# Softmax denominators of a two-layer graph attention kernel: summed over queries in the exp's accumulator instead of over keys by accumulating transfers

## The chip, the cores and the metric

One core of a Trainium2 chip runs the whole program. Times are microseconds of device time; the time of a kernel is the median of its runs. TensorE, VectorE, ScalarE, GpSimd and the sync engine each work through their own queue in order and wait for one another by semaphores.

## The reference

The input is x, 16 graphs of 1024 nodes with 256 features, and an integer adjacency of 1024 x 1024 for each graph, symmetric and with ones on the diagonal. Two layers follow, each added to its input. The first, cut to what matters here:

```python
normed = layer_norm(x, gamma1, beta1)                       # h = relu(layernorm(x)) comes in as x
qkv = normed.reshape(b_, n_, H, HD).transpose(0, 2, 1, 3)   # 8 heads of 32
scores = jnp.einsum('bhqd,bhkd->bhqk', qkv, qkv) * scale
masked = jnp.where(adj_matrix[:, None, :, :] > 0, scores, -jnp.inf)
attn = jax.nn.softmax(masked, axis=-1)
out = jnp.einsum('bhqk,bhkd->bhqd', attn, qkv)
x = x + out
return x + gelu(layer_norm(x, gamma2, beta2) @ W1 + b1) @ W2 + b2
```

Queries, keys and values are the same array, so the scores are symmetric, and with a symmetric adjacency the masked scores are too. The second layer is a graph attention with one head (leaky ReLU of bilinear logits, masked, softmax, weighing, two projections, ELU). Only the first layer's softmax is touched by the change.

## The kernel before, in words

All is float32 but the masks (fp8). There is a fast path, written out in `fast_path`, and a `general_path` that runs afterwards only if flags gathered on the chip (`seen`, `dens`, `not_bounded`) say that the fast path's assumptions did not hold. The fast path leaves out the maximum of the softmax.

*Attention of the first layer* (`attention`, L969). Each graph is a batch b of 32 blocks, in the order query half qh (2 of 512 queries), group g (2 of four heads), key tile kt (8 of 128 keys). `scores` (L974) puts keys on the partitions and queries on the free axis: for a block, sixteen small matmuls (L990) fill two PSUM tiles of 128 x 1024, one for two heads. VectorE adds the mask and moves each tile to SBUF (L1011), ScalarE takes the exp in place (L1014), one instruction of 1024 elements per tile. In batch 0 TensorE adds the mask of the first tile itself (matmuls with an identity, L571), and ScalarE reads that tile from PSUM. One block later `weigh` (L1022) multiplies by the values (L1027) into one PSUM tile `o` of 128 (four heads of 32 features) x 512 queries, gathered over the eight key tiles.

*Denominators.* The sum that is needed for a query runs over keys, that is, over partitions and key tiles. The e tiles of key tile 0 are kept as accumulators (`acc`), and for the others `add_up` (L1048) issues a transfer from GpSimd's queue that adds e to acc in SBUF (L1051). In batch 0 the odd key tiles are summed apart by VectorE (L1038). After the last key tile, `total` (L924) sums acc over the partitions with matmuls by ones (L929), ScalarE copies the sums out (L937), `invert` (L942) turns them by small matmuls (L947) so that queries lie on the partitions, and VectorE takes reciprocals (L951). `finish` (L954) then transposes the weighed values (L961), multiplies by the reciprocals (L963), and GpSimd adds the result to the residual h (L967). `go_on` (L1068) moves these steps on by one each block through the lists `weighed`, `summed` and `totalled`.

*The rest of a batch* (`rest`, L1114: the MLP with its Gelu, the second layer, the stores) is a chain of generators that run during the attention of the next batch, so that TensorE always alternates between attention blocks and pieces of the previous batch. Its 128-wide matmuls go through `matmul` (L566), which splits the stationary operand into four quarters of 32 columns.

*What sets the order.* The order of instructions on each engine is written out in Python. Streams (L1435 to L1492) each yield a place on a common axis, in batches (one block is 1/32), and the loop at L1494 always runs the stream with the smallest place. `clock` is a planned time in microseconds; `defer` (L758) puts an instruction behind others by a due time on that clock, and `turns` holds transposes that wait for a free PSUM tile (`make_turns`, L913). `stream_p` prepares the first statistics for the MLP (`prepare`, L1092), `stream_m` loads and transposes the masks of a query half before it begins (`turn_masks`, L890). At the end of `fast_path` each engine's instructions are tied to this order.

The line numbers are those of the kernel before. The functions that the diff touches:

Of the kernel before, what the change touches and what calls it, by code (L numbers as in the profile page):

```python
# [12 lines left out]
I32 = mybir.dt.int32  # L13
AF = mybir.ActivationFunctionType
# [480 lines left out]
def fast_path(  # L495
# [54 lines left out]
    ep = pool("ep", 5)  # L550
    accp = pool("accp", 2)
# [36 lines left out]
    def convert_mask(b, t, halves):  # L588

        m = mqp.tile([P, N], FP8, tag="mq", name=f"mq_{b}_{t}")  # L590
        for i, a in enumerate(halves):
            nc.vector.tensor_scalar(
                m[:, i * QW : (i + 1) * QW], a, 0.0, NEG8, op0=ALU.is_le, op1=ALU.mult, saturate=False
            )
        return m
# [4 lines left out]

    each_head = const.tile([P, GH], F32, name="each_head")
    nc.vector.tensor_copy(each_head, ident[:, ::HD])
# [57 lines left out]
    seen = const.tile([P, 4], F32, name="seen")  # L660
# [114 lines left out]
    def prologue(b, st):  # L775
# [61 lines left out]
        if b == 0:  # L837
# [3 lines left out]
            mqs = midp.tile([P, 2 * TPH, N], FP8, tag="mid", name="mq_0")  # L841
# [48 lines left out]
    def turn_masks(b, qh, st):  # L890
# [7 lines left out]
        mq = convert_mask(*raw)  # L898
        raw = fetch_mask(b, ts[1])
        for i in range(TPH):  # L900
            yield
            nc.sync.dma_start_transpose(pairs[:, :, i * P : (i + 1) * P], mq.bitcast(BF16))
            if i + 1 < TPH:
                mq = convert_mask(*raw)
            if i + 2 < TPH:
                raw = fetch_mask(b, ts[i + 2])


# [4 lines left out]
    def make_turns():  # L913
        room = 3 - open_sums[0] - bool(summed or totalled) if open_sums[0] else 100
# [7 lines left out]
    scored, weighed, summed, totalled = [], [], [], []  # L922

    def total(b, qh, g, os, accs):  # L924

        den = ps_tile([P, QW], f"den_{b}_{g}_{qh}")
        for j in range(GH):
            for acc in accs:
                nc.tensor.matmul(  # L929
                    den[j * HD : (j + 1) * HD, :],  # L930
                    ones,
                    acc[j // 2][:, j % 2, :],
                    start=acc is accs[0],
                    stop=acc is accs[-1],
                )
        ds = tmpp.tile([P, QW], F32, tag="w2", bufs=3, name=f"ds_{b}_{g}_{qh}")
        nc.scalar.copy(ds, den)  # L937
        totalled.append((b, qh, g, ds, os))

    finished = {}  # L940

    def invert(b, qh, g, ds, os):  # L942

        pt = ps_tile([P, TPH, GH], f"ptds_{b}_{g}_{qh}")
        for t in range(TPH):
            for c in range(0, P, HD):
                nc.tensor.matmul(  # L947
                    pt[c : c + HD, t, :], ds[:, t * P + c : t * P + c + HD], each_head, start=True, stop=True
                )
        rl = smallp.tile([P, TPH, GH], F32, tag="rl", name=f"rl_{b}_{g}_{qh}")  # L950
        ready = defer(1.0, lambda: nc.vector.reciprocal(rl, pt))  # L951
        turns.append((1, lambda: finish(b, qh, g, rl, ready, os)))

    def finish(b, qh, g, rl, ready, os):  # L954
# [7 lines left out]
        ot = tmpp.tile([P, TPH, GH, HD], F32, tag="w2", bufs=3, name=f"ot_{b}_{g}_{qh}")  # L962
# [6 lines left out]
    def attention(b, st):  # L969
        va, kT = st["va"], st["kT"]  # L970

        def scores(qh, g, kt):  # L974
# [24 lines left out]
            if b == 0 and kt % 2:  # L999

                odd = midp.tile([P, 2, 2, QW], F32, tag="mid", name=f"odd_{g}_{qh}_{kt}")
            for i in range(2):
                if b == 0 and kt % 2:
                    e = odd[:, i]
                elif kt == 0:
                    e = accp.tile([P, 2, QW], F32, tag=f"acc{i}", name=f"acc_{b}_{g}_{qh}_{i}")
                else:
                    e = ep.tile([P, 2, QW], F32, tag="e", name=f"e_{b}_{g}_{qh}_{kt}_{i}")
# [5 lines left out]
                weights = lambda e=e, masked=masked: nc.scalar.activation(e, masked, AF.Exp, scale=SCALE)  # L1014
# [4 lines left out]
        acc = {}  # L1019


        def weigh(qh, g, kt, es):  # L1022
# [11 lines left out]
            if b == 0 and kt % 2:  # L1034

                if kt > 1:
                    for n, (e, w) in enumerate(zip(es, odds[g, qh])):
                        defer(1.0 + 2.5 * n, lambda e=e, w=w: nc.vector.tensor_add(e, e, w))  # L1038
                odds[g, qh] = es
            if kt == NT - 1:  # L1040
                c = tmpp.tile([P, QW], F32, tag="w2", bufs=3, name=f"os_{b}_{g}_{qh}")
                nc.vector.tensor_copy(c, o)
                weighed.append((b, qh, g, c, [s[g, qh] for s in (sums, odds) if s]))

        sums, odds = {}, {}


        def add_up(qh, g, kt, e, i):  # L1048
            if b == 0 and kt % 2:
                return  # L1050
            nc.gpsimd.dma_start(sums[g, qh][i], e, accum_op=ALU.add)  # L1051

        units = [(qh, g, kt) for qh in range(NQH) for g in range(NG) for kt in range(NT)]
        for u in units:
# [3 lines left out]
            rest_of_weights()  # L1058
            qh, g, kt = u
            if kt == 0:  # L1060
                sums[g, qh] = es
            else:
                for i in range(2):
                    defer(2.0 + 1.5 * i, lambda u=u, e=es[i], i=i: add_up(*u, e, i))
            scored.append((weigh, (*u, es)))
            yield

    def go_on():  # L1068
        was_weighed, was_summed, was_totalled = weighed[:], summed[:], totalled[:]
        for l in (weighed, summed, totalled):  # L1070
            l.clear()
# [493 lines left out]
```

## Time and profile before

| | us |
|---|---|
| median of 3 runs | 3475.63 (3471.41 to 3486.16) |
| the profiled execution, own time | 3465.53 |
| its span, first to last instruction | 3463.8 |
| TensorE busy | 3421.5 |
| VectorE busy | 2751.4 |
| ScalarE busy | 1857.5 |
| GpSimd busy | 1416.9 |
| accumulating transfers L1051: 864, 453 MB | GpSimd 756.2 |
| exps L1014, 128 x 1024: 852 on e, the others on acc or in batch 0 | 1.057 each |
| scores L990 and weighing L1027 (8192 and 4096 matmuls) | 577.3 and about 550 |
| summing L929 and turning L947 of the denominators (544 and 2048 matmuls) | 76.0 and 29.8 |

The profile is of one execution. An engine's busy time is the union of its instructions' durations. TensorE's durations overlap and their ends are modelled, so its price for a piece of work is better read from start to start in the timeline, where each row has its start, its length, engine, line, output and inputs, shape and count, and in brackets the idle time before it with what ended it. PEld is TensorE's loading of weights, which runs beside its matmuls. The granted TensorE clock was 0.998 of full speed. Batch 0's attention lies between 22 and 146 us, and from batch 1 on a batch takes about 211 us.

### The profile page before, as it was taken

What the parts mean: (1) busy time and instruction counts of PE and PEld (TensorE: products, weight loads), DVE (VectorE), ACT (ScalarE), POOL (GpSimd) and SP (SyncE); (2) the same over time, 40 slices, a digit from 0 to 9 for tenths busy, and PEclk for the clock granted to TensorE, in tenths of its full rate; (3) what the DMA queues carried; (4) which work ended last, traced back from release to release, by engine and by line L of the source; (5) the groups of instructions that cost most, each with busy time, mean ns of one, the idle gap of its engine ahead of it and who ended that gap; (6) DMA issues with size and microseconds to landing.
All of it is one profiled execution on the core that took longest, in us unless ns stands there. A gap on an engine that the chain in (4) does not pass through costs nothing. (4 is left out here: it accounts for less than half of the span.)

```text
span 3463.8 us, 119015 instructions
## 1 busy us (share of the span) xinstructions
PE 3421.5 (99%) x52478; PEld 1644.7 (47%) x52478; DVE 2751.4 (79%) x5194; ACT 1857.5 (54%) x2184; POOL 1416.9 (41%) x1708
## 2 busy tenths in 40 slices
PE   7999999999999999999999999999999999999998
PEld 2344444444444444444444444444444444444477
DVE  6888788787878878888887887878878788887754
ACT  5555555555555555555555555555555555555522
POOL 4443443434444344443444434344343443433220
PEclk9999999999999999999999999999999999999999
DMA  8799989999899998999999899998999989899730
GB/s 195 154 183 181 185 164 194 177 193 185 164 185 176 185 187 169 184 171 191 189 177 186 166 189 179 188 187 168 186 178 193 186 163 184 170 193 180 153 64 14
DMA packets 281902, 598.56 MB, mean 173 GB/s; under 512 B 94880, under 2 KB 130080, under 8 KB 281376
## 3 DMA queue, kind: packets, MB, share of 16 engines
q0 software_dynamic: 124416, 453.04, 71.5%
q1 hardware_dynamic: 156672, 137.56, 15.9%
q8 instruction: 414, 6.78, 0.8%
q14 instruction: 112, 0.92, 0.1%
q10 hardware_dynamic: 288, 0.26, 0.0%
HBM read 104.21 MB, written 16.78 MB: 35 GB/s over the span
## 5 line engine op out<-in xcount | busy, mean ns | idle before, releaser
L1014 ACT ACTIVATE e<-e 128x1024 f32<-128x1024 f32 x852 | 895.9, 1057 | 947.6 <-DVE e L1011 715.3
L1051 POOL DMA_DIRECT2D acc<-e x864 | 756.2, 891 | 1447.4 <-DMA acc<-e 664.6
L1011 DVE TENSOR_TENSOR e<-s,mk 128x1024 f32<-128x1024 f32 x852 | 1004.0, 1218 | 180.1 <-PE s L990 148.4
L990 PE MATMUL s<-kT 32*64 32x512 f32 x8192 | 577.3, 615 | 2.9 <-DVE odd L1011 2.9
L1027 PE MATMUL o<-e,va 128*32 128x512 f32 x3456 | 462.9, 606 | 2.1 <-ACT e L1014 2.1
L571 PE MATMUL pa<-gw,e 128*32 128x258 f32 x7648 | 454.3, 380 | 0.6 <-issue 0.6
L571 PE MATMUL lg<-fT,uT 128*32 128x256 f32 x7680 | 448.5, 379 | 0.0
L571 PE MATMUL ph<-yT,w 128*32 128x256 f32 x7808 | 448.5, 379 | 0.0
L571 PE MATMUL po<-w,hid 128*32 128x256 f32 x7680 | 440.5, 379 | 0.0
L571 PEld LDWEIGHTS ph<-yT,w 128*32 128x32 f32 x7808 | 259.8, 110 | 197.7 <-issue 42.5
L571 PEld LDWEIGHTS po<-w,hid 128*32 128x32 f32 x7680 | 250.2, 110 | 209.1 <-issue 61.6
L571 PEld LDWEIGHTS lg<-fT,uT 128*32 128x32 f32 x7680 | 258.4, 110 | 190.1 <-issue 38.9
L571 PEld LDWEIGHTS pa<-gw,e 128*32 128x32 f32 x7648 | 249.9, 110 | 202.5 <-issue 49.9
L1287 ACT ACTIVATE e<-e,shift 128x512 f32<-128x512 f32 x256 | 183.0, 717 | 186.0 <-DVE e L1286 161.2
L1281 DVE SCALAR_TENSOR_TENSOR e<-lg,gw,mk 128x256 f32<-128x256 f32 x512 | 223.2, 478 | 71.6 <-PE lg L571 61.1
L1184 DVE TENSOR_TENSOR hid<-ph,b1c 128x512 f32<-128x512 f32 x256 | 175.6, 688 | 85.6 <-PE ph L571 74.2
L1027 PEld LDWEIGHTS o<-e,va 128*32 128x32 f32 x3456 | 68.8, 108 | 354.0 <-issue 219.9
L1286 DVE SCALAR_TENSOR_TENSOR e<-e 128x512 f32<-128x512 f32 x256 | 196.6, 768 | 8.8
L1014 ACT ACTIVATE acc<-acc 128x1024 f32<-128x1024 f32 x124 | 131.0, 1057 | 129.0 <-DVE acc L1011 124.6
L990 PEld LDWEIGHTS s<-kT 32*64 32x64 f32 x8192 | 120.6, 130 | 162.8 <-issue 105.0
L1011 DVE TENSOR_TENSOR acc<-s,mk 128x1024 f32<-128x1024 f32 x124 | 146.1, 1218 | 20.8 <-PE s L990 20.6
L815 POOL TENSOR_TENSOR nrm<-nrm,g 128x256 f32<-128x256 f32 x128 | 113.3, 885 | 60.9 <-DVE nrm L749 60.9
(146 smaller groups left out, 3817.9 us busy)
## 6 DMA issues: line engine op xcount, KB each, us to landing
acc<-e POOLq DMA_DIRECT2D x864, 512.0 KB, 6.2
adj<-in_adj_dram SPq DMA_DIRECT2D x248, 256.0 KB, 5.6
h<-in_x_dram SPq DMA_DIRECT2D x64, 256.0 KB, 6.3
xb<-in_x_dram SPq DMA_DIRECT2D x128, 128.0 KB, 4.2
out_dram<-z SPq DMA_DIRECT2D x128, 128.0 KB, 4.0
adj<-in_adj_dram SPq DMA_DIRECT2D x4, 512.0 KB, 7.1
mk<-mq SPq DMA_TRANSPOSE x128, 6.4
w<-in_L_gnn_W_dram SPq DMA_DIRECT2D x2, 1024.0 KB, 9.6
```

The lines of the kernel that those rows point to most:

```text
L571: nc.tensor.matmul(out[c : c + HD], lhsT[:, c : c + HD], rhs, start=start, stop=stop)
L815: nc.gpsimd.tensor_mul(nrm, nrm, g1)
L990: nc.tensor.matmul(sc[j // 2][c : c + P // 2, j % 2, :], kT[r, g, kt * P + c : kt * P + c + P // 2], kT[r, g, qs], start=j >= by_pe, stop= ...
L1011: nc.vector.tensor_tensor(e, masked, mb, op=ALU.add)
L1014: weights = lambda e=e, masked=masked: nc.scalar.activation(e, masked, AF.Exp, scale=SCALE)
L1027: nc.tensor.matmul(o[j * HD : (j + 1) * HD, :], va[:, kt, (g * GH + j) * HD : (g * GH + j + 1) * HD], es[j // 2][:, j % 2, :], start=(kt = ...
L1051: nc.gpsimd.dma_start(sums[g, qh][i], e, accum_op=ALU.add)
L1184: nc.vector.tensor_tensor(hid[:, f0 : f0 + 2, :], ph, b1c[:, f0 : f0 + 2].unsqueeze(2).to_broadcast([P, 2, CW]), op=ALU.add,)
L1281: nc.vector.scalar_tensor_tensor(e[:, j, :], lg[:, j, :], gw[:, kt, D : D + 1], st[c // 2][:, kt // 2, qs, kt % 2], op0=ALU.add, op1=ALU.add,)
L1286: nc.vector.scalar_tensor_tensor(e, e, ALPHA, e, op0=ALU.mult, op1=ALU.max)
L1287: ready = defer(2.5, lambda: nc.scalar.activation(e, e, AF.Exp, bias=shift))
```

## The change

*Sums over queries.* Because the masked scores are symmetric, the denominator of node n is also the sum over all queries of row n, with n as a key. A row is a partition of an e tile, and its sum over 512 queries is what ScalarE's accumulator can give with the exp. The exp of a tile (two heads) is therefore cut into two instructions of 512 elements, one for each head, with `accum_out` into a column of a new tile `den` (one per batch: query half, key tile, head). `total`, `add_up`, the acc tiles, the odd sums of batch 0 and the matmuls of `invert` are gone. The new `invert` adds the two query halves' columns on VectorE and takes reciprocals. As a node's sum needs both query halves, the finishes of the first query half now come in the second one: for each group, after its key tiles 3 and 7 of the second half, `invert` handles the nodes of query half 0 and 1, and `close` puts `finish` on the list of turns. The weighed values of the first half are kept until then (`w2`, 3 buffers to 5).

*Check of symmetry.* `turn_masks` keeps the fp8 masks with queries on the partitions (`mq`) beside the transposed ones (`mk`). `compare_masks` subtracts one from the other on GpSimd, for the pairs of tiles on and under the diagonal of query halves, 12 instructions of 128 x 512 per batch; VectorE ORs the bits of each result into `uneven` as int32 (128 x 256). At the end the maximum byte of `uneven` goes into the flags, and a difference leads to `general_path`. `stream_k` sets the compares' places: from 0.02 to 0.20 of a batch after each query half begins.

*Places and rooms.* `prepare` moves from 0.85 and 0.90 to 0.91 and 0.935, the start of `rest` from 0.94 to 0.96 and its run from 0.98 to 0.99; the last batch closes in two steps instead of four; e tiles get 6 buffers instead of 5 and the accumulators' four go.

```diff
-    ep = pool("ep", 5)
-    accp = pool("accp", 2)
+    ep = pool("ep", 6)
+    denp = pool("denp", 2)
...
+    seen = const.tile([P, 6], F32, name="seen")
+    nc.gpsimd.memset(seen[:, 5:6], 0.0)
+    uneven = const.tile([P, QW // 2], I32, name="uneven")
+    nc.gpsimd.memset(uneven, 0)
...
-        mq = convert_mask(*raw)
+        mq = st["mq", qh] = mqp.tile([P, TPH, N], FP8, tag="mq", name=f"mq_{b}_{qh}")
+        convert_mask(mq[:, 0], *raw)
...
+    def compare_masks(b, qh, st):
+        for half in range(qh + 1):
+            for i in range(TPH):
+                kt = qh * TPH + i
+                odd = smallp.tile([P, QW], BF16, tag="odd", bufs=2, name=f"odd_{b}_{qh}_{half}_{i}")
+                key = st[half][:, kt // 2, :, kt % 2]
+                query = st["mq", qh][:, i, half * QW : (half + 1) * QW]
+                nc.gpsimd.tensor_tensor(
+                    odd.rearrange("p (u v x) -> p u v x", u=2, v=2),
+                    key.rearrange("p (u v x) -> p u v x", u=2, v=2),
+                    query.rearrange("p (u x v) -> p u v x", u=2, v=2),
+                    op=ALU.subtract,
+                )
+                o = odd.bitcast(I32)
+                defer(3.0, lambda o=o: nc.vector.tensor_tensor(uneven, uneven, o, op=ALU.bitwise_or))
+                yield
...
-        room = 3 - open_sums[0] - bool(summed or totalled) if open_sums[0] else 100
+        room = 3 - open_sums[0] if open_sums[0] else 100
...
-    def total(b, qh, g, os, accs):
...
-                nc.tensor.matmul(
-                    den[j * HD : (j + 1) * HD, :],
-                    ones,
-                    acc[j // 2][:, j % 2, :],
...
-        nc.scalar.copy(ds, den)
...
-    def invert(b, qh, g, ds, os):
...
-                nc.tensor.matmul(
-                    pt[c : c + HD, t, :], ds[:, t * P + c : t * P + c + HD], each_head, start=True, stop=True
-                )
...
-                weights = lambda e=e, masked=masked: nc.scalar.activation(e, masked, AF.Exp, scale=SCALE)
+                def weights(e=e, masked=masked, i=i):
+                    for j in range(2):
+                        n = g * GH + 2 * i + j
+                        nc.scalar.activation(
+                            e[:, j], masked[:, j], AF.Exp, scale=SCALE, accum_out=den[:, qh, kt, n : n + 1]
+                        )
...
-                        defer(1.0 + 2.5 * n, lambda e=e, w=w: nc.vector.tensor_add(e, e, w))
...
-            nc.gpsimd.dma_start(sums[g, qh][i], e, accum_op=ALU.add)
+        def close(qh, g):
+            turns.append((1, lambda: finish(b, qh, g, *rl[g, qh], os[g, qh])))
+        def invert(qh, g):
+            r = smallp.tile([P, TPH, GH], F32, tag="rl", name=f"rl_{b}_{g}_{qh}")
+            ts, hs_ = slice(qh * TPH, (qh + 1) * TPH), slice(g * GH, (g + 1) * GH)
+            def f():
+                nc.vector.tensor_tensor(r, den[:, 0, ts, hs_], den[:, 1, ts, hs_], op=ALU.add)
+                nc.vector.reciprocal(r, r)
+            rl[g, qh] = r, defer(2.5, f)
...
+            if qh == NQH - 1 and kt % TPH == TPH - 1:
+                invert(kt // TPH, g)
+                if kt < NT - 1:
+                    close(kt // TPH, g)
...
-        for _ in range(4):
+        for _ in range(2):
...
-            place = b + 0.98
+            place = b + 0.99
...
-                yield b + 0.85 + 0.05 * c
+                yield b + 0.91 + 0.025 * c
...
-            yield b + 0.94
+            yield b + 0.96
...
+    def stream_k():
+        for b in range(B):
+            for qh in range(NQH):
+                yield from spread(
+                    compare_masks(b, qh, states[b]), TPH * (qh + 1), b + 0.5 * qh + 0.02, b + 0.5 * qh + 0.2
+                )
```

## The prediction, made before the changed kernel ran

> **What bounds the kernel now.** I read the page's shares first. TensorE is busy 99% of the span, and the slices show it so from the second one to the last but one.
>
> ```profile
> PE 3421.5 (99%) x52478; PEld 1644.7 (47%) x52478; DVE 2751.4 (79%) x5194; ACT 1857.5 (54%) x2184; POOL 1416.9 (41%) x1708
> PE   7999999999999999999999999999999999999998
> ```
>
> A busy TensorE could still be one that waits inside modelled durations, so I went to the timeline and measured from start to start. Over all runs of matmuls of one kind followed by the same next kind, smallest and median distance agree (scores L990 to the weighing L1027: 1.044 us in both, over 511 places). The excess over the median adds up to 21 us in the whole program, 16 of it before 165 us, that is in batch 0. From batch 1 on TensorE waits for nobody: what is taken off its queue shortens the program, and what is added elsewhere is free until it uses up a slack. These rows of the timeline in mid-program price the work that goes:
>
> ```profile
> 1686.60 1.06 PE L1027 MATMUL o<-e,va 128*32 128x512 f32 x8
> ...
> 1687.49 1.04 PE L929 MATMUL den<-acc,ones 128*32 128x512 f32 x8
> ...
> 1688.35 1.91 PE L571 MATMUL po<-w,hid 128*32 128x256 f32 x32
> ...
> 1694.68 1.07 PE L1027 MATMUL o<-e,va 128*32 128x512 f32 x8
> ...
> 1695.57 0.42 PE L947 MATMUL ptds<-each_head,ds 128*32 128x4 f32 x30
> ...
> 1695.86 3.64 PE L571 MATMUL ph<-yT,w 128*32 128x256 f32 x62
> ```
>
> The denominators' sum (L929) holds the queue from 1687.49 to 1688.35, 0.86 us; turning them (L947) from 1695.57 to 1695.86, 0.29 us. In both cases the weighing before keeps its own 0.88 us.
>
> The slack that the change spends is that between the last exp of a block (one query half, one group of four heads, one key tile) and its weighing. The tightest place repeats in every batch; here it is once, in block 28 of 32 of a batch:
>
> ```profile
> 1810.24 2.35 DVE L1011 TENSOR_TENSOR e<-s,mk 128x1024 f32<-128x1024 f32 x2
> ...
> 1811.54 2.19 ACT L1014 ACTIVATE e<-e 128x1024 f32<-128x1024 f32 x2 [3.31 <-DVE e L1011]
> ...
> 1814.11 0.16 PEld L1027 LDWEIGHTS o<-e,va 128*32 128x32 f32 x8 [0.81 <-ACT e L1014]
> ```
>
> The exps end at 1813.73, the weighing starts 0.4 us later. I took this distance for all 480 blocks of batches 1 to 15: median 2.3 us, a tenth under 0.45 us (blocks 28 and 29 about 0.4, block 21 0.65, block 6, behind a Gelu and its table load, 0.8). The scores' own slack (VectorE's mask add, L1011, frees their PSUM tile) has a median of 2.6 us.
>
> **What the Trainium skill says.** ScalarE: Activation LUTs, section What ACT_TABLE_LOAD costs, gives an activation with immediate scale and bias as 186 ns + 0.833 ns per element, and back-to-back ones as overlapping by about 93 ns. The trace agrees: 1057 ns for 1024 elements (1039 by the page), and neighbours overlap by about 100 ns. The same page, What it computes, names an accumulator output, but no price. GPSIMD Engine Reference, section 3.1, has a two-input elementwise operation at about 2.6 cycles per element at 1.2 GHz; for 512 elements that is an estimate of 1.1 us and a start. L967, 128x512, takes 1.45 us on average here, 1.29 in the median. SBUF — State Buffer, section Who interferes with whom, says that a VectorE instruction with two SBUF inputs and a GpSimd instruction that reads SBUF hold one another up for the whole instruction. L1286, of that kind, shows it: shortest 691 ns, mean 768.
>
> **The change part by part.**
> *TensorE.* L929 has 512 + 32 matmuls, 68 groups of eight: 68 x 0.86 = 58.5 us. L947 happens 64 times: 64 x 0.285 = 18.2 us. Together 77 us, all on the path. I don't use the page's busy sums (70.6 + 5.4 + 29.8 = 106), because they count overlapping ends twice. Everything else on TensorE stays.
> *ScalarE.* 1024 exps over 1024 elements become 2048 over 512, each with an accumulator output, and 64 copies L937 (36 us) go. A half costs 1057 - 512 x 0.833 = 630 ns, or 0.53 from start to start. Reading the accumulator has no row: from below nothing, from above one smallest instruction, the 128x1 copies of L693 at 159 ns, without any overlap and with a little for the write, 0.2 us. I take 0.06 per half (159 less the overlap of 100), and the full 0.16 after the last. A block's four halves then end 0.63 + 3 x 0.59 + 0.16 = 2.56 us after the first begins, against 2.0 to 2.19 now: about 0.5 us later. Against the slack of the 480 blocks, 0.5 us makes 7 us of waits, mostly in blocks 28 and 29; blocks that lose L929 become shorter, for which I add 3: +10 us. ScalarE's busy time rises by some 1024 x (4 x 0.59 / 2 - 1.0) less 36, to about 2.0 ms of 3.4, so it isn't the bound.
> *GpSimd and the DMA queues.* The 864 accumulating transfers (L1051, 0.88 us each on GpSimd's queue, 453 MB, 71.5% of the DMA engines) go: worth nothing directly, since TensorE waited for them for 1.4 us in all. What they hid or crowded only gets earlier. In come 192 compares, 128x512 with fp8 inputs and four-dimensional patterns. No such row is there; I take L967's 1.3 to 1.5 us and keep 0.7 (the 128x256 rows) and 5 us as ends. GpSimd falls from 1417 us to 1417 - 757 + 192 x 1.45 = 940.
> *VectorE.* In: 192 ORs of 128x256, L1333's 496 ns, 95 us; 64 adds of 128x16 beside the 64 reciprocals that stay, at L951's 248 ns, 16 us. Out: 24 adds L1038, 30 us. Net +81, to 2832 us of about 3400 (83%). The OR is a new wait: behind it stand the mask adds, and behind these the exps and TensorE. It is put 3 us of planned time after its compare, and in most places several VectorE instructions lie between. The ORs fall into blocks 1 to 7 and 17 to 23, of which 3, 6 and 21 have under 1.1 us of slack: I put 0.4 us for each of 15 batches, +6 us; bounds 0 and 95 (every OR on the path).
> *Moved.* The first query half's finishes (four transposes, 0.59 us of TensorE; L963, 0.68 of VectorE; L967, 1.45 of GpSimd) go to blocks 20 and 28, the second's to 25 and to block 1 of the next batch, now without the steps of summing and turning in between. The first MLP statistics go from 0.85 and 0.90 of a batch to 0.91 and 0.935; the next stage's two x loads on the sync queue go with it from 0.94 to 0.96. A finish at block 28 leaves one block (about 6 us) for 0.66 + 0.68 + 1.45 = 2.8 us, and statistics and normalizing have two more before their transposes: nothing; if that cover were gone, at most the 2.8 us once per batch. The new add of the two halves' sums waits on VectorE for the block's last exp; 2.5 to 3.3 us of other VectorE work stand between mask add and this add: nothing.
> *Batch 0.* Here exps read PSUM directly, and TensorE's next block waits for them: half exps cost up to 0.4 x 32 = 13 us. Against that, 30 us of VectorE adds and the transfers disappear, and 16 us of present waits with them at best. I set it to nothing, bounds -16 to +13.
> Sum: -77 + 10 + 6 + 0 = -61 us. The profiled execution took 3465.5 us (span 3463.8), so 3404.5; the runs shown have a median of 3475.6, 0.29% above it, which gives 3414 us.
>
> **Rivals.**
> 1. *ScalarE's accumulator is dear.* At 0.83 us per half (0.63 + 0.2, no overlap) the block's exps end 1.1 us later, and the same slacks give 39 us of waits; with batch 0 at its worse end: -77 + 39 + 6 + 13 = -19, 3457 us on the runs' scale. For it: no row prices that read. Against: the 128x1 row is only 159 ns.
> 2. *Slower: VectorE waits for GpSimd's compares.* Place: the second half of each batch's attention, where eight compares are spread over some six blocks. In seven blocks there (46 us in the trace) GpSimd has 16 us of work besides the transfers, which leaves 30 us, 3.7 per compare. Beyond that each OR stops VectorE, with all mask adds behind it. At 5 us per compare: 8 x 1.3 = 10.4 us a batch, less 2.3 of slack, x 15 = +120, so -77 + 10 + 120 + 6 = +59, 3535 us. It decides from about 4.5 us per compare. For: unpriced types and patterns. Against: L967's 1.29 us for as many elements.
> 3. *All of it and more.* Nothing of ScalarE shows, and batch 0's waits vanish: -77 - 16 = -93, 3382 us.
> 4. *The compare doesn't recognise the symmetry*, and the general path runs as well: thousands of us. The two patterns name the same pairs when I work them out, so 1%.
>
> **How the numbers follow.** Chances: forecast 0.60, dear accumulator 0.18, slower by the compares 0.11, more than the sum 0.10, general path 0.01. A measurement of this kernel tells about 0.5% from no change, 17 us. Faster: 0.60 + 0.10 and the better half of rival 1, 0.80; same: the rest of rival 1, 0.08; slower 0.12. The range runs from near rival 3 to just past rival 1: 3386 to 3462.
>
> **What would show it.** No L929 or L947, weighing followed after 0.88 us by the next kind everywhere. Half exps of 0.6 to 0.65 us with a small row between; if their distance from start to start exceeds 0.75 us, rival 1 gains, and waits of the weighing on ScalarE appear in blocks 28, 29 and 21. Compares over 3.7 us, or VectorE idle before the OR for GpSimd, would mean rival 2. It is wrong at the root if TensorE, with these 77 us gone, shows new gaps in every block.

## The result, and the profile after

The changed kernel takes 3421.8 us (median of 4 runs, 3421.3 to 3422.7); the kernel before 3473.9 us (3471.4 to 3486.2, the three runs given above and one more beside the changed kernel). The ratio is 0.984, with a 95% interval of 0.982 to 0.987. The forecast was 3414 us in a range of 3386 to 3462. The profiled execution took 3422.06 us against 3465.53 before: 43.5 us less, where the sum promised 61. So the sign and the size came out, but the sum is 17.5 us short.

TensorE stays the bound. These two lines of the page after answer to those of before:

```profile
PE 3356.2 (98%) x49790; PEld 1603.4 (47%) x49790; DVE 2799.1 (82%) x5427; ACT 2061.6 (60%) x5192; POOL 880.6 (26%) x1038
PE   6899999999999999999999999999999999999998
```

There are 2688 fewer matmuls and 65 us less of busy time, but 98% instead of 99%: a little idle time has come in. ScalarE and VectorE came out near the forecast (2.0 ms and 2832 us), GpSimd somewhat below it (940).

The weighing is followed after 0.88 us by the next kind, with no sum in between (timeline after, the last weighing of batch 8):

```profile
1811.14 1.06 PE L1022 MATMUL o<-e,va 128*32 128x512 f32 x8
...
1812.02 3.64 PE L572 MATMUL ph<-yT,w 128*32 128x256 f32 x64
```

The half exps are as costed. This is block 28 again, the tight place shown of before:

```profile
1787.07 2.35 DVE L1000 TENSOR_TENSOR e<-s,mk 128x1024 f32<-128x1024 f32 x2
1788.38 0.63 ACT L1007 ACTIVATE e<-e 128x512 f32<-128x512 f32 x1 [3.88 <-DVE e L1000]
1788.91 0.19 ACT L1007 ACTIVATION_READ_ACCUMULATOR e<-e 128x1 f32 x1
1789.01 0.61 ACT L1007 ACTIVATE e<-e 128x512 f32<-128x512 f32 x1
...
1790.75 0.19 ACT L1007 ACTIVATION_READ_ACCUMULATOR e<-e 128x1 f32 x1
1791.43 0.16 PEld L1022 LDWEIGHTS o<-e,va 128*32 128x32 f32 x8 [0.81 <-ACT e L1007]
```

From 1788.38 to the end of the last read at 1790.94 are 2.56 us, to the hundredth what I had put, though by parts that offset each other: a half starts 0.61 us after the one before, where I had put 0.59, and less is left after the last start. The read of the accumulator is a row of its own (187 ns), but its first half lies under the exp before it and the rest under the next one.

To see where the time went I compared start to start: from the first scores of a batch to those of the next.

| stretch (profiled executions) | before | after | difference | by the sum |
|---|---|---|---|---|
| batch 0 | 123.3 us | 118.9 us | -4.4 | about -6 (three sums and turnings) |
| one later batch (median) | 210.83 us | 208.65 us | -2.18 | -4.55 from TensorE, +1.07 from ScalarE and the ORs |
| last block to the end | 162.9 us | 161.1 us | -1.8 | about -1 |

TensorE's own part is there: in batch 9 the sum takes 3.43 us less and the turning 1.12, together the 4.55. But other kinds take 2.1 us more, and most of it stands in three blocks; against the shortest time that each has in the runs below, block 0 is 0.5 us longer, block 19 1.0 and block 22 0.65. There TensorE waits for PSUM tiles (the tiles that its matmuls write) that ScalarE empties (uT L1234, gw L1249), for VectorE's copy of the outputs (L1031), or for mask adds.

### The profile page after: what moved, and what is told of

The parts are those of the page before. It is cut to its first block, busy times and chain, and to the rows that moved or that the text cites. A ratio compares the mean times of both kernels' runs of the same rounds, so it can differ in the third digit from the quotient of the medians.

```text
span 3420.3 us, 114618 instructions
## 1 busy us (share of the span) xinstructions
PE 3356.2 (98%) x49790; PEld 1603.4 (47%) x49790; DVE 2799.1 (82%) x5427; ACT 2061.6 (60%) x5192; POOL 880.6 (26%) x1038
## 5 line engine op out<-in xcount | busy, mean ns | idle before, releaser
L1007 ACT ACTIVATE e<-e 128x512 f32<-128x512 f32 x1984 | 1224.8, 619 | 960.5 <-DVE e L1000 958.1
L1000 DVE TENSOR_TENSOR e<-s,mk 128x1024 f32<-128x1024 f32 x992 | 1168.1, 1218 | 195.2 <-PE s L987 192.7
L1022 PE MATMUL o<-e,va 128*32 128x512 f32 x4096 | 557.5, 606 | 1.3 <-ACT e L1007 1.3
L1007 ACT ACTIVATION_READ_ACCUMULATOR e<-e 128x1 f32 x1984 | 371.2, 187 | 0.0
L1022 PEld LDWEIGHTS o<-e,va 128*32 128x32 f32 x4096 | 83.6, 108 | 424.6 <-issue 198.9
L964 POOL TENSOR_TENSOR h<-h,ot 128x512 f32<-128x512 f32 x64 | 84.7, 1323 | 697.8 <-DVE ot L960 697.8
L917 POOL TENSOR_TENSOR odd<-mk,mq 128x512 bf16<-128x512 fp8e5 x192 | 233.3, 1216 | 100.2 <-DVE uneven L924 100.2
L1272 DVE SCALAR_TENSOR_TENSOR e<-e 128x512 f32<-128x512 f32 x256 | 209.5, 818 | 8.8
L744 POOL TENSOR_TENSOR rs_c<-ve_c,mhalf 128x2 f32<-128x2 f32 x64 | 44.5, 695 | 477.4 <-DVE ve_c L742 378.1
```

The costliest lines, as they stand in the source:

```text
L744: nc.gpsimd.tensor_tensor(rs, ve, mhalf[:, :nt], op=ALU.pow)
L917: nc.gpsimd.tensor_tensor(odd.rearrange("p (u v x) -> p u v x", u=2, v=2), key.rearrange("p (u v x) -> p u v x", u=2, v=2), query.rearrang ...
L964: nc.gpsimd.tensor_add(ho, ho, ot.rearrange("p t j d -> p t (j d)"))
L1000: nc.vector.tensor_tensor(e, masked, mb, op=ALU.add)
L1007: nc.scalar.activation(e[:, j], masked[:, j], AF.Exp, scale=SCALE, accum_out=den[:, qh, kt, n : n + 1])
L1022: nc.tensor.matmul(o[j * HD : (j + 1) * HD, :], va[:, kt, (g * GH + j) * HD : (g * GH + j + 1) * HD], es[j // 2][:, j % 2, :], start=(kt = ...
```

## The experiments

My first theory (A) was that the longer exps do this: ScalarE empties the PSUM tiles from the same queue, behind four half exps. Its rivals were the compares and ORs (B), the new places (C), and a TensorE term that was too large (D). Line numbers are those of each run's own kernel: the leaky maximum of the second attention, L1272 after, is L1259, L1270 or L1278 in the others.

**Without compares and ORs.** `compare_masks` only yields; the rest of the kernel stays, and the symmetry is not looked at.

```
         for half in range(qh + 1):
             for i in range(TPH):
...
-                nc.gpsimd.tensor_tensor(
...
-                defer(3.0, lambda o=o: nc.vector.tensor_tensor(uneven, uneven, o, op=ALU.bitwise_or))
                 yield
```

> The changed kernel (3421.8 us) without the 192 GpSimd compares and the 192 VectorE ORs; the result word stays at its initial zero, so the adjacency's symmetry is not looked at. The sum promised 61 us and 52 came; from batch 1 on 36 came where TensorE's part alone is 68, so some 32 us were given back. Theory A (the longer exps keep ScalarE from emptying PSUM tiles, and TensorE waits for these tiles): the compares have little to do with it, 3416 to 3422 us. Theory B (the ORs, 103 us of VectorE, push the mask adds and the copies behind them): most of the 32 us comes back, 3390 to 3400. Theory C (the new places of the finishes and statistics cost it): 3418 to 3422.

Measured: 3389.7 us (3388.4 to 3390.0), 32 us below after. That is more than the 17.5 us that the sum is short, because the rest of the change had gained more than was put (the table further down), and it comes from where A said that little was to be had. Batch 0 falls from 118.9 to 113.6 us, a batch from 208.65 to 206.83. A fell as the main cause.

**Whole exps without accumulator, and halves without accumulator.** Both leave the denominators out (a constant tile is read in their place). The edit of the first is shown; the second keeps the loop over the two halves and only drops `accum_out`.

```
-                    for j in range(2):
-                        n = g * GH + 2 * i + j
-                        nc.scalar.activation(
-                            e[:, j], masked[:, j], AF.Exp, scale=SCALE, accum_out=den[:, qh, kt, n : n + 1]
-                        )
+                    nc.scalar.activation(e, masked, AF.Exp, scale=SCALE)
```

> The changed kernel with each exp again over 1024 elements and without accumulator output: 1024 instead of 2048 instructions and no accumulator reads. The denominators are left out: a constant stands in their place, read by the same adds and reciprocals. Everything else is as after. Theory A: the blocks' exps end some 0.4 us earlier and ScalarE empties PSUM tiles in time; 25 to 34 us below after, 3388 to 3397 us. Theory B: 3416 to 3422. Theory C: 3416 to 3422, since the finishes stay where they are. If it comes out between, at 3400 to 3412, ScalarE has a part and so has another cause.

> The changed kernel with the exps in halves of 512 elements, but without accumulator output (the denominators are left out, a constant stands in their place). It parts the splitting from the reading of the accumulator. A half would start 0.53 us after the one before instead of 0.61, a block of four end after 2.2 us instead of 2.56 (whole ones: 2.1). Theory A, if the reads are what costs: within 5 us of the kernel with whole exps, 3388 to 3402 us. Theory A, if the split itself costs: 3412 to 3422. Theories B and C: 3416 to 3422, like after.

Measured: 3412.6 us (3410.7 to 3414.6) with whole exps, 3416.5 us (3415.5 to 3416.7) with halves. So beside the compares the exps' new form costs 9 us, about 4 for the split and 5 for the reads; the forecast had put 10. A has a part, but far from the 25 us that it would need. Halves without the read start 0.54 us apart, with it 0.61.

**The kernel before, without TensorE's sums.** The matmuls of `total` and `invert` are left out, and with them the denominators; ScalarE's copy reads the accumulated tile itself, and the accumulating transfers stay.

```
-                nc.tensor.matmul(
-                    den[j * HD : (j + 1) * HD, :],
...
-        nc.scalar.copy(ds, den)
+        nc.scalar.copy(ds, accs[-1][0][:, 0, :])
...
-        pt = ps_tile([P, TPH, GH], f"ptds_{b}_{g}_{qh}")
+        pt = ds[:, : TPH * GH].rearrange("p (t j) -> p t j", j=GH)
...
-        ready = defer(1.0, lambda: nc.vector.reciprocal(rl, pt))
+        ready = defer(1.0, lambda: nc.vector.tensor_scalar(rl, pt, 0.0, 1.0e-4, op0=ALU.mult, op1=ALU.add))
```

> The kernel before (3473.9 us) without TensorE's two steps for the denominators: the 544 matmuls of the sum and the turning by small matmuls are left out, the copy on ScalarE reads the accumulated tile itself, one VectorE instruction of the same shape stands for the reciprocal, and the accumulating transfers stay. So the denominators are left out. It measures the term of 77 us by itself. If the term is right: 73 to 80 us below before, 3394 to 3401 us. If the term was too large, because the queue closes up less than the rows say (theory D: the missing 32 us lie in it): 40 to 50 us, 3424 to 3434.

Measured: 3426.6 us, 46 us below before, with runs from 3419.9 to 3435.4. By the number D is right, by the trace it isn't: undisturbed batches take 206.2 to 206.5 us, 4.4 to 4.6 less than before, as sized. Others take up to 213. The waits say why; first the kernel before, then this one (engine, line, what it waited for: total us, times, longest):

```profile
DVE e L1011 <- DMA acc<-e: 4.2, 8, 0.9
```

```profile
DVE e L996 <- DMA acc<-e: 44.4, 33, 4.1
```

With TensorE faster, the accumulating transfers don't keep pace, and the mask add waits for an exp tile that a transfer still reads. I had called the end of the transfers worth nothing because TensorE waited 1.4 us for them. It is worth nothing only while TensorE is slow enough to hide them; with the transfers still there, a good part of the 77 us is not earned. Not all of the shortfall need be theirs: in the two longest batches, 9 and 10 (213.3 us each), the granted clock of TensorE also stands at 0.5 for 3.4 and for 6.8 us; in the kernel before it does so only in batch 0 and at the very end.

**Compares alone, ORs alone.** The first experiment had taken away two things. With compares alone, the line with `defer` shown there goes and nothing else: the results are left unread. With ORs alone, the compare goes, and each OR reads a constant zero tile. Neither checks the symmetry.

```
-                defer(3.0, lambda o=o: nc.vector.tensor_tensor(uneven, uneven, o, op=ALU.bitwise_or))
+                defer(3.0, lambda: nc.vector.tensor_tensor(uneven, uneven, none, op=ALU.bitwise_or))
```

> The changed kernel with the 192 GpSimd compares but without the 192 ORs (the compares' results are left unread, so the symmetry is not checked). Taking both away gave 32 us (3389.7). Theory B1 (the ORs themselves cost it: 192 x 0.42 us in blocks whose VectorE has no room): 3389 to 3396 us, block 22 as short as without the compares (6.96 us). Theory B2 (the compares hold up VectorE's two-input instructions, as L1276 with 22 us more than without them shows): 3400 to 3412 us, block 0 and batch 0 stay long (6.55 and 118.9 us), block 22 gets shorter.

> The changed kernel with the 192 ORs but without the compares: each OR reads a constant zero tile instead (so the symmetry is not checked). Theory B1: VectorE has the same number of instructions, 3412 to 3422 us. Theory B2: an OR takes 0.42 us everywhere and nothing is held up; 3396 to 3408 us, with block 0 at 6.08 and batch 0 near 113.6 us. If both parts cost, this run's distance to 3389.7 and that of the run with compares alone add up to about 32 us; if they only cost together, both stay below 3396.

Measured: 3418.5 us (3417.6 to 3421.0) with compares alone, 3390.8 us (3388.5 to 3391.9) with ORs alone. B2 names the right part, but both runs lie outside its windows: the compares cost more than it said, and the ORs less. The 192 ORs that I had budgeted on VectorE's queue cost 1 us; the 192 compares, on an engine that is busy for a quarter of the time, cost 29. The 2 us that are left come only with both together, in batch 0: it takes 118.9 us after, 114.9 with compares alone and 113.2 with ORs alone, while batches 1 to 14 take 2921.6, 2921.5 and 2893.1 us. The same place with and without them shows how. First without compares and ORs, at the end of block 18 of batch 9 (this block's successor starts at 1909.29):

```profile
1904.74 0.17 DVE L742 TENSOR_SCALAR ve_b<-mv_b 128x2 f32<-128x2 f32 x1
...
1907.98 0.69 DVE L1259 SCALAR_TENSOR_TENSOR e<-e 128x512 f32<-128x512 f32 x1
...
1908.59 0.15 DVE L796 SCALAR_TENSOR_TENSOR nm<-mv_a,rs_a 128x2 f32<-128x2 f32 x1
...
1909.21 1.08 ACT L801 ACTIVATE h<-h,nm,rs_a 128x256 f32<-128x256 f32 x2
...
1910.19 0.67 ACT L1221 ACTIVATE uT<-puT,w_a 128x512 f32<-128x512 f32 x1
...
1910.91 0.13 PEld L572 LDWEIGHTS pg<-wo,fT 128*32 128x32 f32 x4 [0.41 <-ACT uT L1221]
```

And with compares alone (the successor starts at 1926.69):

```profile
1922.14 0.62 DVE L742 TENSOR_SCALAR ve_b<-mv_b 128x2 f32<-128x2 f32 x1
...
1923.51 3.41 POOL L917 TENSOR_TENSOR odd<-mk,mq 128x512 bf16<-128x512 fp8e5 x3
...
1925.84 1.63 DVE L1270 SCALAR_TENSOR_TENSOR e<-e 128x512 f32<-128x512 f32 x1
...
1927.39 0.15 DVE L796 SCALAR_TENSOR_TENSOR nm<-mv_a,rs_a 128x2 f32<-128x2 f32 x1
...
1927.57 1.09 ACT L801 ACTIVATE h<-h,nm,rs_a 128x256 f32<-128x256 f32 x2 [0.41 <-DVE nm L796]
...
1928.57 0.67 ACT L1232 ACTIVATE uT<-puT,w_a 128x512 f32<-128x512 f32 x1
...
1929.29 0.59 PEld L572 LDWEIGHTS pg<-wo,fT 128*32 128x32 f32 x16 [1.40 <-ACT uT L1232]
```

Three compares run one behind the other. The leaky maximum (two inputs, both from SBUF, where all tiles on the chip but the PSUM tiles lie) takes 1.63 instead of 0.69 us; it ends 0.55 us after the third compare, as if its work had begun only then. The small ve_b ahead of it, beside an earlier compare (1921.58 to 1922.74), had already put VectorE's queue 0.45 us back. Behind it on VectorE stands the small nm, behind that on ScalarE the h of the next batch, behind that the emptying of uT, and TensorE waits for that tile 1.40 instead of 0.41 us. Four instructions on two engines lie between the compare and TensorE's wait, and the wait bears ScalarE's name: that had led me to theory A. Block 19, to which this wait belongs, takes 7.57 us, 0.99 more than without compares.

The whole trace says the same. With compares alone, 57 of the 256 leaky maxima overlap a compare in time, and their median is 1.55 us; that of the other 199 is 0.69. Of the mask adds, which read PSUM, 95 overlap a compare, and their median is 1.21 us, against 1.22. Ahead of block 0 of batch 9 one maximum is held by 0.53 us; everything behind it on VectorE comes that much later, and so does the copy of the outputs (L1029) that TensorE waits for. That block takes 6.36 instead of 6.08 us, and 6.60 in the median over batches 1 to 14. A rival is that the compares delay other work in GpSimd's own queue. From batch 1 on, only one wait of TensorE for GpSimd is new against the kernel without compares, in block 18 (weight loads of ptk, 10.9 us in all), and that block keeps its 7.79 us; VectorE's waits for GpSimd grow by 1.6 us in the whole program.

This is the hold-up of the Trainium skill, SBUF — State Buffer, section Who interferes with whom, which the prediction itself cites. I quoted it and gave it no price.

**Half as many ORs.** Results in 8 bits, two compares in one tile, one OR for both.

```
-                odd = smallp.tile([P, QW], BF16, tag="odd", bufs=2, name=f"odd_{b}_{qh}_{half}_{i}")
+                if i % 2 == 0:
+                    odd = smallp.tile([P, 2, QW], FP8, tag="odd", bufs=2, name=f"odd_{b}_{qh}_{half}_{i}")
...
+                if i % 2:
+                    o = odd.rearrange("p i q -> p (i q)").bitcast(I32)
+                    defer(3.0, lambda o=o: nc.vector.tensor_tensor(uneven, uneven, o, op=ALU.bitwise_or))
```

> The changed kernel with the compares' results in 8 instead of 16 bits, two in one tile, and one OR for each two compares: 96 ORs of the same 128x256 words instead of 192, all of the check kept. Theory B1: half of the ORs' cost comes back, 3404 to 3410 us. Theory B2: the 192 compares still hold up VectorE; only the ORs' own hold-ups halve, 3410 to 3418 us.

Measured: 3426.2 us (3425.7 to 3427.7), slower than after by 4 us, outside both expectations. That the number of ORs isn't what costs agrees with the run before; a batch takes 209.03 us, with block 18 0.7 us longer than after. Why it is longer I didn't follow up. A compare into 8 bits takes the same 1.16 us as one into 16.

**All compares where VectorE has room.** `stream_k` puts them into blocks 1 to 10.

```
+                yield from spread(compare_masks(b - 1, 1, states[b - 1]), 2 * TPH, b + 0.03, b + 0.17)
+                yield from spread(compare_masks(b, 0, states[b]), TPH, b + 0.19, b + 0.3)
```

> The changed kernel with all twelve compares of a batch, and their ORs, in blocks 1 to 10 (those of the second half of a batch a half batch later, in the next one), since VectorE is busy for only 3.8 of 7.0, 4.3 of 6.4, 4.2 of 7.2 and 4.9 of 7.2 us in blocks 1, 2, 7 and 10, and for 6.5 of 7.0 in block 22. Theory B (the place decides: what VectorE gets in blocks that are full is added to the block): 3393 to 3403 us. If the place doesn't matter, because each OR and each compare costs TensorE wherever it is: 3417 to 3425 us.

Measured: 3411.6 us (3409.9 to 3412.2). That is between the two expectations. Blocks 19 and 22 are short again, but block 0 keeps its 0.55 us, block 5 gets 0.3, and the last batch's compares lengthen the end by 5.6 us. Other instructions are held there: the normalizing y<-h L748 goes from 53.9 to 73.9 us in all, z<-z,en from 60.2 to 72.8. Room on VectorE alone is not the measure; it also counts which VectorE instruction runs while a compare does.

**Compares in step with the mask adds.** The mask add takes one operand from PSUM, and none was ever held (1.22 us on average, with compares or without). One result tile instead of two makes each compare wait for the OR before it; that OR goes directly ahead of the two mask adds, one compare a block, in blocks 1 to 4 and 17 to 24. All of the check stays.

```
-                odd = smallp.tile([P, QW], BF16, tag="odd", bufs=2, name=f"odd_{b}_{qh}_{half}_{i}")
+                odd = smallp.tile([P, QW], BF16, tag="odd", bufs=1, name=f"odd_{b}_{qh}_{half}_{i}")
...
-                defer(3.0, lambda o=o: nc.vector.tensor_tensor(uneven, uneven, o, op=ALU.bitwise_or))
+                ors.append(lambda o=o: nc.vector.tensor_tensor(uneven, uneven, o, op=ALU.bitwise_or))
...
             es = []
+            if ors and (qh * NG + g) * NT + kt in slots[qh]:
+                ors.pop()()
```

> The changed kernel with all of the check, but each compare made to start with a mask add: one result tile instead of two, so that a compare waits for the OR before it, and that OR is put directly ahead of the block's two mask adds, which take 2.4 us and read one operand from PSUM. One compare in each of blocks 1 to 4 and 17 to 24. The compares alone had cost 29 of the 32 us, the ORs alone 1. Theory B2 (what costs is a VectorE instruction held for as long as a compare that runs beside it, 691 ns becoming 1629): the mask adds aren't held, the leaky maximum (128x1024) keeps to 0.69 to 0.73 us on average and block 22 to 6.96; 3389 to 3397 us. Theory B3 (what costs is the 1.16 us that each compare takes in GpSimd's queue, ahead of the statistics and normalizing that others wait for): no better than after, 3415 to 3430, and GpSimd's waits for the OR make it worse.

Measured: 3398.6 us (3398.1 to 3401.2), 23 us below after; 0.978 of before (0.977 to 0.980). It misses B2's window by 2 us, and B3 is far off: GpSimd does the same compares in about the same time (229 us for 233). Only 27 of the 256 leaky maxima overlap a compare now, and 238 mask adds do, with a median of 1.22 us. The edit also gives the compares other blocks; no run parts what these places alone are worth from what the mask adds' cover is worth. The timeline, again in block 18 of batch 9, has the compare under the mask adds, and the leaky maximum free:

```profile
1912.85 0.42 DVE L927 TENSOR_TENSOR uneven<-uneven,odd 128x256 int32<-128x256 int32 x1
...
1913.18 2.35 DVE L1006 TENSOR_TENSOR e<-s,mk 128x1024 f32<-128x1024 f32 x2
1913.80 1.16 POOL L920 TENSOR_TENSOR odd<-mk,mq 128x512 bf16<-128x512 fp8e5 x1
...
1916.35 0.69 DVE L1278 SCALAR_TENSOR_TENSOR e<-e 128x512 f32<-128x512 f32 x1
```

The groups of VectorE (busy us, mean ns) show the same over the whole program, first after, then in step:

```profile
L1272 DVE SCALAR_TENSOR_TENSOR e<-e 128x512 f32<-128x512 f32 x256 | 209.5, 818 | 8.8
L924 DVE TENSOR_TENSOR uneven<-uneven,odd 128x256 int32<-128x256 int32 x192 | 103.3, 538 | 1.8
L742 DVE TENSOR_SCALAR ve_b<-mv_b 128x2 f32<-128x2 f32 x64 | 17.4, 272 | 2.2
```

```profile
L1278 DVE SCALAR_TENSOR_TENSOR e<-e 128x512 f32<-128x512 f32 x256 | 194.5, 760 | 8.8
L927 DVE TENSOR_TENSOR uneven<-uneven,odd 128x256 int32<-128x256 int32 x192 | 82.3, 428 | 5.9 <-POOL odd L920 5.6
L742 DVE TENSOR_SCALAR ve_b<-mv_b 128x2 f32<-128x2 f32 x64 | 11.5, 180 | 2.2
```

Without compares the leaky maximum has 187.1 us and ve_b 11.5. The last row, with one tensor input of two elements, is held as well; the same section of the skill says that tensor_scalar can contend with GpSimd in a two-port mode. Whether ve_b ran in that mode no run shows; that a compare holds it the two timelines above do (0.62 for 0.17 us).

**TensorE's term alone.** Without compares and ORs and with whole exps, as in the two kernels above (symmetry and denominators left out).

> The changed kernel without compares and ORs, and with whole exps without accumulator output (a constant stands for the denominators, and the symmetry is not checked). What remains of the change is TensorE's term, the transfers that are gone and the new places. If the costs are separate and add up: 3389.7 less 9.2 = 3380 us, with a period of 206.3 us per batch (210.83 less 4.55). If ScalarE's and the compares' waits hide one another, below that isn't possible in the period, and it is 3383 to 3388 us. If the new places cost something of their own: over 207 us per batch, above 3389 us.

Measured: 3376.1 us (3374.0 to 3378.6), and 206.19 us per batch from the second on. That is 4 us less than the expected sum. In the ordinary batch the costs add up: 206.19, with ScalarE's half exps 206.83 (+0.64), with the compares 208.65 (+1.82). In batch 0 they don't: the half exps cost 3.7 us there without compares (109.9 to 113.6) and 0.7 beside them (118.2 to 118.9). The new places cost nothing that can be seen in the ordinary batch, where 210.83 less 4.55 is 206.28; no run moves them back by themselves.

**The kernel before, without the transfers.** `add_up` is left out; the sums cover only the first key tile, so the denominators are left out.

```
-                for i in range(2):
-                    defer(2.0 + 1.5 * i, lambda u=u, e=es[i], i=i: add_up(*u, e, i))
```

> The kernel before without its 864 accumulating transfers; the sums by TensorE, their copies and turnings stay, but sum only the first key tile (and batch 0's odd tiles), so the denominators are left out, and one VectorE instruction of the same shape stands for the reciprocal. The kernel before without TensorE's sums came out at 3426.6 with single batches up to 7 us long and runs 15 us apart. If the transfers cost nothing in the kernel before, as I put it: 3464 to 3474 us, like before. If the waits for them are what differs from run to run and from batch to batch: 3455 to 3464 us, all runs within 4 us, and all batches from the second on at 210.8 us.

Measured: 3455.8 us (3451.8 to 3456.9), beside 3474.4 us for the kernel before: 19 us in the medians, 9 in the profiled executions. Every batch from batch 2 on takes 210.8 to 211.1 us. The gain is in batch 0 (123.3 to 120.4 us) and in single batches of before that were up to 3 us longer, not in the ordinary batch, where the transfers were indeed hidden.

**Two more edits.** In batch 0 the compares go to later blocks; of the gw tiles, the one of key tile 6 is copied by VectorE.

```
+    slots = {b: ((1, 2, 3, 4) if b else (8, 9, 11, 12), (17, 18, 19, 20, 21, 22, 23, 24)) for b in range(B)}
...
-            (nc.vector.tensor_copy if t % 2 else nc.scalar.copy)(gw[:, t, : D + 1], pg[:, : D + 1])
+            (nc.vector.tensor_copy if t % 2 or t == 6 else nc.scalar.copy)(gw[:, t, : D + 1], pg[:, : D + 1])
```

> The kernel whose compares start with the mask adds (3398.6 us), with two more edits against what is left there. In batch 0 the compares go to blocks 8, 9, 11 and 12, because there the OR in block 2 waits for a compare whose masks are late, and block 3 takes 7.85 instead of 4.61 us. And the one copy of the gw tiles that stands on ScalarE behind four half exps in block 19 (L1255, key tile 6) goes to VectorE, which has 1.4 us without work there: TensorE waits for it, 12.2 us in the program, and block 19 takes 6.91 us against 6.10 without compares and with whole exps. Theory A2 (ScalarE's longer exps delay a PSUM tile just there): block 19 at 6.1 to 6.3, 15 x 0.7 = 10 us, with batch 0's 3: 3383 to 3388 us. If block 19 waits for something else: only batch 0's part, 3394 to 3397 us. If VectorE has no room for the copy: 3397 to 3405 us.

Measured: 3395.2 us (3394.5 to 3395.6), 0.978 of before (0.976 to 0.980): the fastest here that does all of the work. But only batch 0's part came (117.5 to 115.6 us). Block 19 did get 0.45 us shorter, and block 22 as much longer. In block 22 (it starts at 1932.29) a compare again runs outside the mask adds, and the leaky maximum beside it is held:

```profile
1937.23 1.16 POOL L920 TENSOR_TENSOR odd<-mk,mq 128x512 bf16<-128x512 fp8e5 x1
...
1937.50 1.44 DVE L1278 SCALAR_TENSOR_TENSOR e<-e 128x512 f32<-128x512 f32 x1
```

The OR that should time it had run before the mask adds of 1934.27; between them and this compare GpSimd was busy normalizing. The compare keeps step only while nothing else stands in GpSimd's queue.

## Why the prediction came out where it did

All numbers in this table are differences of profiled executions, so they add up; the last line is their sum.

| step | put | measured | from |
|---|---|---|---|
| TensorE's sums and turnings, with transfers and VectorE's adds gone | -77 (and 0 for the rest) | -91.3 | 3465.5 to 3374.2 |
| half exps with accumulator | +10 | +14.2 | 3374.2 to 3388.4 |
| ORs, and compares beside them | +6 and 0 | +33.6 | 3388.4 to 3422.1 |
| sum | -61 | -43.5 | |

*TensorE.* Right: 4.55 us per batch put, 4.64 found. Of the 14 us more, half is the extra gain that rival 3 described: batch 0 goes from 123.3 to 109.9 us, 7 more than its share of the sums. Batches 1 to 14 give 7 more than the 4.55 us put for each, since batch 1 is shorter and the long single batches of before are gone. What I had passed over in the mean clock of 0.998: within batch 0 of before, the granted clock is 0.5 for 6.8 us from 77.2 on and for 3.4 us from 138.6 on; a block's scores at 79.87 need 1.94 us to the weighing there, instead of 1.04. With TensorE's term alone the clock is 0.5 nowhere but at the very end. Half of these 10.2 us, an estimate of 5 us, is part of batch 0's gain. I had put batch 0 at nothing, which held only with the compares' 5.3 us and the half exps' 3.7 in it again.

*ScalarE.* Right in mechanism and nearly in size, with 0.61 us from start to start for 0.59. In the ordinary batch it costs 0.64 us, 9.6 in fifteen. The place was another: I looked for it in blocks 28, 29 and 21, where the exp's end is near the weighing; it stands in blocks 16 and 19, where ScalarE empties PSUM tiles between exps.

*GpSimd and VectorE.* This is the step of the sum that failed, in the sentence "The OR is a new wait: behind it stand the mask adds", for which I put 6 us. The ORs alone cost 1. I priced the compares at 1.3 to 1.5 us each (measured: 1.16 in the median) and put GpSimd's busy time at 940 us (881), neither of them too low, and concluded that an engine with so much free time costs nothing. The term that was missing is what a compare does to a VectorE instruction beside it: 22 us on the leaky maximum, 21 on the ORs (103.3 against 82.3 when they run in step), 6 on ve_b, together about 50 us of VectorE's time in blocks of which some have none to spare. That the OR's upper bound of 95 us covers the 33.6 is luck. Block 22 of batch 9, in the trace after, has both:

```profile
1948.21 1.17 POOL L917 TENSOR_TENSOR odd<-mk,mq 128x512 bf16<-128x512 fp8e5 x1
1948.27 1.65 DVE L1272 SCALAR_TENSOR_TENSOR e<-e 128x512 f32<-128x512 f32 x1
...
1952.03 1.29 PE L987 MATMUL s<-kT 32*64 32x512 f32 x16
...
1952.11 1.92 DVE L924 TENSOR_TENSOR uneven<-uneven,odd 128x256 int32<-128x256 int32 x2
...
1952.60 1.16 POOL L917 TENSOR_TENSOR odd<-mk,mq 128x512 bf16<-128x512 fp8e5 x1 [3.22 <-DVE uneven L924]
...
1955.44 2.35 DVE L1000 TENSOR_TENSOR e<-s,mk 128x1024 f32<-128x1024 f32 x2
```

The maximum takes 1.65 us, and of two ORs (0.42 us each where nothing disturbs them) one takes 1.4, because the next compare starts as soon as the first OR has freed its tile. The mask adds come 3.4 us after the block's scores; without compares and ORs it is 1.65.

*Rivals.* Rival 2 named the right pair of engines, the wrong mechanism (VectorE waiting for a compare's result) and a threshold of 4.5 us per compare; with 1.16 us the harm was done almost without such waits: VectorE's idle time before all 192 ORs is 1.8 us. Rival 1 had too high a price for the read. Of the signs that I gave, the last one came nearest: new gaps did appear, though in three blocks and not in every one.

*From the profile to the runs.* I added 0.29% because the runs of before lie above their profile. The runs of after don't (3421.3 to 3422.7 around 3422.1). Without the transfers the kernel before varies by 5 us instead of 15, so that distance was probably theirs and went with them. These 10 us (3404.5 to 3414) cover more than half of the 17.5 by which the sum was short. So it is partly luck that the forecast came within 8 us: by step it was off by 14 us one way and by 4 and 28 the other, and the surcharge took off 10 of what was left.

## What to carry to other kernels

An engine with free time is not free: before work is moved to GpSimd, list the VectorE instructions that will run beside it and take two inputs from SBUF, and those of the tensor_scalar kind with one such input (ve_b and y<-h here), and price each at up to the whole GpSimd instruction. Where the work must stay there, tie its start to a VectorE instruction that reads PSUM; here that brought 23 us, the change of places included. And when a wait bears an engine's name, follow that engine's queue back to the first instruction that is longer than its shortest case; here it was the leaky maximum, the fourth back, on another engine.

## What was new of the hardware

- The accumulator output of an exp is a second row of 187 ns, but it adds only 0.07 us from start to start (0.54 to 0.61 us for 512 elements).
- GpSimd's subtraction of two fp8 tiles of 128x512 in four-dimensional patterns takes 1.16 us in the median, less than its 128x512 addition in f32 (1.28), and the same with 8 and with 16 bits out.
- A two-element tensor_scalar on VectorE beside a compare took 0.62 us instead of 0.17 (ve_b, in the kernel with compares alone). In the same trace these were not held beside a compare: the logits' scalar_tensor_tensor that reads PSUM (L1265, 62 times, 0.47 us), the addition to ph, also from PSUM (L1168, 15 times, 0.69), and the batch statistics of one SBUF tile (L739, 42 times, 0.39).
